# Depthwise convolution begun one stage earlier, with five small moves in the order of the chains

## The chip, the cores and the metric

The kernel runs on one core of a Trainium2 chip. The metric is the time of one execution on the device in microseconds, as the median of several runs. The core has TensorE (PE in the profile), VectorE (DVE), ScalarE (ACT), GpSimd (POOL) and the queue engine SyncE (SP); GpSimd and SyncE do almost nothing here but issue DMA transfers. Each engine works through its own queue in order and waits on semaphores that the others raise.

## The reference

Eight images `x` of 384 channels and 32 x 32 positions go through two layers, all in float32. The first is an attention block on the 1024 positions as tokens, the second a convolution block.

```python
# layer 0, xf = x as (B, 1024, 384)
xn  = layernorm(xf, g1, beta1)
q, k, v = heads(einsum('bnc,oc->bno', xn, w_qkv) + b_qkv)      # 8 heads of 48
out = softmax(q @ k.T * 48 ** -0.5) @ v
x1  = einsum('bnc,oc->bno', out, w_proj) + b_proj + xf
h   = gelu(einsum('bnc,oc->bno', layernorm(x1, g2, beta2), w_fc1) + b_fc1)   # 1536 wide
x2  = x1 + einsum('bnh,oh->bno', h, w_fc2) + b_fc2
# layer 1
y   = depthwise_conv_7x7(x2, dw_w) + dw_b
y   = gelu(layernorm(y, ln_w, ln_b) @ w1 + b1)                  # 1536 wide
gx  = sqrt(sum(y ** 2, positions)); nx = gx / (mean(gx, channels) + 1e-6)
y   = grn_gamma * (y * nx) + grn_beta + y
out = x2 + y @ w2 + b2
```

## The kernel before, in words

The 384 channels of an image lie on the partitions as three channel tiles (`ct` 0 to 2) of 128; the 1024 positions are the free axis, cut in halves of 512 columns, since a matmul writes one 512-column bank of the accumulators. The 1536 hidden channels are 12 tiles `m`.

**The order of TensorE's work.** Image `b` goes through `qk` (queries and keys), attention of its first query half, `proj`, attention of the second query half, fc1 on the first half of the positions, `proj` of the second half, the rest of fc1, fc2; then comes w1 of image `b - 1`, v of image `b + 1`, and w2 of image `b - 1`. So while the matmuls of image `b`'s attention run, the depthwise convolution of image `b - 1` is computed beside them, on VectorE and ScalarE. Image 0 has extra work on the weights (`prepare`, `forms`, `folds`), and image 7 an ending of its own.

**Products of thirds.** `qk`, w1 and part of fc1 use a scheme with fewer products: a group is three output tiles by two column halves, made of 15 products instead of 18, with copies on ScalarE and additions on VectorE between them (`tiles_by_thirds`: matmul L456, ScalarE copies L469 and L477, VectorE additions L472 and L475). w1 has four such groups of 512 columns per image (`grn_up`, tiles `h_*`); fc1 has two groups of 256 columns in the first half of images 2 to 6, called fast (`gelu_group`, tiles `fc_*`; the first covers m = 6 to 8, the second 9 to 11). Their right-hand sides are sums of blocks of the normalised input, made on VectorE (`make_thirds`, L430). fc2 and w2 use a similar scheme on larger sums (`by_thirds`: L485, VectorE L1055, L1052).

**fc1 of a fast image.** First group, m = 0 and 1, `proj` of the second query half, then m = 2 to 5, the second group, and the twelve tiles of the second half of the positions (L404, gelu on ScalarE L497). Ahead of the second group lie the second layernorm's steps for the second half of the positions (`layernorm`: VectorE L540 and L543, a matmul with ones L507, VectorE L550, squares on ScalarE L557, VectorE L561 and L564, L507 again, ScalarE L577 and L578, VectorE L581). ScalarE changes its function table (ACT_TABLE_LOAD, L493 or with L497) between L577's logarithm and a gelu. Products of 256 columns leave a 128x256 tile of the accumulators.

**The convolution** of an image is 49 taps for each channel tile. `convolution` puts one tap of one channel tile after another on VectorE (L1205 for the first tap with its bias, L1207 for the others: `acc = window * weight + acc`); the window is a shifted view of the padded image `pad`, which ScalarE fills by copies of x (L965). `help_convolution` gives the last 6, 7 and 7 taps of the three tiles to ScalarE (L1228) and adds them to `acc` by a DMA that GpSimd issues (L1229). `start_conv` starts both after w1's stage; `conv_norm` and `end_soon` start the third layernorm (`ln3_*`, two halves side by side, `abreast`; sums on 64-row strips, L521) on `acc` in fc1's second half, and `before_fc2` lets `make_thirds` follow. `norm_of_next` normalises the next image (`ln1_*`: sums L1918, VectorE L1938, ScalarE L1940, last scaling L1964).

**What sets the order.** Nothing is scheduled at run time: the Python code writes each engine's queue. `Flow` keeps a clock that every matmul advances by its cost (`U = 0.857` for 512 columns). The side work is written as generators (chains) that yield a wait; once the clock has passed a chain's due time, its next step is put into the queues behind what stands there. A `paced` chain counts its waits from its last due time, others from the present; `flow.finish` emits the rest of a chain at once. `hold` makes the convolution pause while the named stages run. So each number that a chain yields is a place in the queues, not a time on the chip:

```python
start_conv(b, 1.65 if b == B - 2 else 1.95, (23, 2.4), (24, 9.0), (25, 20.0), (84, 1.45))
```

This says 2.4 per tap up to the 23rd tap, 9.0 after the 24th, 20.0 after the 25th, 1.45 up to the 84th and 1.95 from there.

**Buffers.** Ring `p` has three tiles of 128 x 1024, used by attention's probabilities (L812), fc2's and w2's `e` tiles and the squares of w1's stage (`waste`); ring `res` has four tiles of 128 x 512. The accumulators are two double banks (`s_tile`) and four single ones in rotation (`o_tile`); the sums L507 and L521, half of L1918's and fc1's matmuls draw from the four.

**Weights** that image 0 prepares are written to device memory (`s_fc`, `s_fc2`, `s_w1`, `s_w2`) and read back by SP's queue (L328); `weights.release()` lets the loads of the finished ones be issued. The same queue moves attention's sums and their inverses (`average`: L764, L768, L771, L773, L790).

Of the kernel before, what the change touches and what calls it, by code (L numbers as in the profile page):

```python
# [46 lines left out]
F32 = mybir.dt.float32  # L47
# [18 lines left out]
NC = HT // CM  # L66
U = 0.857
HELPED = 6, 7, 7
SCALE = HD ** -0.5
EPS0, EPS1, GRN_EPS = 1e-5, 1e-6, 1e-6  # L70
SUM_LOW, SUM_HIGH = 1e-25, 1e25
# [104 lines left out]
def block_kernel(  # L176
# [42 lines left out]
    def half(h):  # L219
        return slice(h * NH, (h + 1) * NH)  # L220
# [305 lines left out]
    def layernorm(src, dst, h, eps, g, name, switch, spare=None, spaced=False, slow=1.0, fold=None, wait=3.4, gentle=False, late=0, lag=0, fold_squares=True):  # L526

        cols = h if isinstance(h, slice) else half(h)
        if isinstance(h, slice):
            h = h.start
        width = cols.stop - cols.start
        if spare:
            a, *squares = (t[:, :width] for t in spare())
            rstd = a
        else:
            a = one.tile([P, NH], F32, tag="ln_a", name=f"{name}_a{h}")[:, :width]
        nc.vector.tensor_tensor(a, src[:, 0, cols], src[:, 1, cols], ALU.add)  # L540
        if gentle:
            yield 1.2
        nc.vector.tensor_tensor(a, a, src[:, 2, cols], ALU.add)  # L543
        yield 2.6 * slow
        totals = yield from token_sums(a, f"{name}_sum{h}", fold, wait)
        yield 0.8
        for ct in range(CT):
            for total, part in totals:
                to, of = dst[:, ct, cols][:, part], src[:, ct, cols][:, part]
                nc.vector.scalar_tensor_tensor(to, total, -1.0 / C, of, ALU.mult, ALU.add)  # L550
            if gentle:
                yield 1.2
        yield 0.8 * slow + lag
        if not spare:
            squares = [three.tile([P, NH], F32, tag="ln_sq", name=f"{name}_sq{h}_{ct}")[:, :width] for ct in range(CT)]
        for ct in range(CT):
            nc.scalar.activation(squares[ct], dst[:, ct, cols], AF.Square)  # L557
            if spaced:
                yield 1.7
        yield 0.8 if spaced else 1.8 * slow  # L560
        nc.vector.tensor_tensor(squares[0], squares[0], squares[1], ALU.add)  # L561
        if gentle:
            yield 1.2
        nc.vector.tensor_tensor(squares[0], squares[0], squares[2], ALU.add)  # L564
        yield 1.8 * slow
        if not fold_squares:
            fold = None
            yield wait
        totals = yield from token_sums(squares[0], f"{name}_var{h}", fold, wait)
        yield 0.8  # L570

        if not spare:
            rstd = one.tile([P, NH], F32, tag="ln_rstd", name=f"{name}_rstd{h}")[:, :width]
        if switch:
            ln_table()
        for var, part in totals:
            nc.scalar.activation(rstd[:, part], var, AF.Ln, bias=eps, scale=1.0 / C)  # L577
        nc.scalar.activation(rstd, rstd, AF.Exp, scale=-0.5)  # L578
        yield (2.6 if switch else 1.2) * slow + late
        for ct in range(CT):  # L580
            nc.vector.scalar_tensor_tensor(dst[:, ct, cols], dst[:, ct, cols], col(g, ct), rstd, ALU.mult, ALU.mult)  # L581
            if gentle and ct < CT - 1:
                yield 1.2
# [338 lines left out]
                    nc.sync.dma_start(out=other, in_=own)  # L922
                proj("x", xt, qt * P // NH)

    def gelu_half(hid, m, h, xn, weights, wname, name, bank=o_tile):
        w = weights.at(wname, m // CM)[:, m % CM * CT : (m % CM + 1) * CT, :]
        ps = linear_half(lambda k: w[:, k, :], lambda k: xn[:, k, :], CT, h, f"{name}_{h}_{m}", bank)
        other_table(hid[:, m, half(h)], ps, AF.Gelu, bias=bfc1[:, m : m + 1])

    def gelu_group(hid, g, b, weights):  # L930

        tiles = {}

# [11 lines left out]
        def behind(n):  # L945
            if n == 14:
                gelu(2)

        c = {f"c{r + 1}{n + 1}": hid[:, 6 + 3 * g + r, quarter(n)] for r in range(CT) for n in range(2)}
        for _ in tiles_by_thirds(weights, f"fc1t_{b}", g, thirds["fc1"], c, bank, behind, U / 2):  # L950
# [27 lines left out]
    def mlp(b, xt, xn, weights, tag, ln, rest, before_fc2=None, behind_ln=None):  # L978
# [9 lines left out]
        for m in range(HT // 2 if fast else HT):  # L988
            if fast and m == 0:
                hold.append("group")  # L990
                gelu_group(hid, 0, b, weights)
                hold.clear()
            gelu_half(hid, m, 0, xn, weights, wa, f"fc1_{b}")
            if m == (1 if fast else 3) and rest:
                rest()
                slow = 0.8 if fast else 1.2 if b == 1 else 1.0
# [2 lines left out]
                ln = flow.spawn(layernorm(xt, xn, 1, eps0, "g2", f"ln2_{b}", True, slow=slow))  # L999
                behind_ln(ln)  # L1000
        if fast:
            gelu_group(hid, 1, b, weights)
            hold.clear()
        flow.finish(ln)
        for m in range(HT):
# [172 lines left out]
        rows, cols = inside(dy, dx, y0, y1)  # L1178
        return 120 + (rows.stop - rows.start) * (cols.stop - cols.start)

    def convolution(acc, us, first=(), y0=0, y1=H, ready=tuple(range(CT)), taken=None, helped=(0,) * CT):

        done = [0] * CT
        ct, n = None, 0
        taps = [KS * KS - k for k in helped]

# [2 lines left out]
        while any(d < k for d, k in zip(done, taps)):  # L1191
            left = [c for c in ready if done[c] < taps[c] and not (taken and taken.get(c, 0) > flow.now)]
            if not left or hold:
                yield 0.5
                continue
            ct = min([c for c in left if c != ct] or left, key=lambda c: done[c])
            i = done[ct]
            share = shares[i]
            dy, dx = divmod(TAPS[i], KS)
            rows, cols = inside(dy, dx, y0, y1)  # L1200
            window = inner(ct)[:, rows.start + dy - PAD : rows.stop + dy - PAD, cols.start + dx - PAD : cols.stop + dx - PAD]
            dst = image(acc[:, ct, :])[:, rows, cols]
            tap = col("dww", ct * KS * KS + TAPS[i])
# [4 lines left out]
            done[ct] += 1  # L1208
            n += 1
            yield share * next((early for m, early in first if n <= m), us)  # L1210

    def help_convolution(acc, us, taken):

# [18 lines left out]
        yield 8.0  # L1232
        taken.clear()

    def grn_up(b, weights, tag):

# [1 line left out]
        y = one.tile([P, HT * N], F32, tag="big", name=f"y_{b}").rearrange("p (m n) -> p m n", m=HT)  # L1240
        gx = small.tile([P, HT], F32, tag="gx", name=f"gx_{b}")
        waste = three.tile([P, N], F32, tag="p", name=f"h_{b}_squares")

        def gelu(g, r):
            m = g + 4 * (r - 1)
# [333 lines left out]
    def prepare(weights, aside):  # L1579
# [117 lines left out]
        if aside:  # L1697
            yield from shift_through_w1()
            return
        yield from forms("fc2", wfc2, s_fc2)  # L1700
        weights.release()
        yield from shift_through_w2()
        yield from forms("w2", w2, s_w2)

# [86 lines left out]
    def main():  # L1791
# [46 lines left out]
        state = {"help": None, "xn": xn, "conv": None, "acc": None, "norm1": None, "norm3": None}  # L1838
        kept = {}

        def start_conv(b, us, *first):
            acc = state["acc"] = one.tile([P, CT, N], F32, tag="acc", name=f"acc_{b}")
            taken = {}
            state["conv"] = flow.spawn(convolution(acc, us, first, taken=taken, helped=HELPED), paced=True)
            state["help"] = flow.spawn(help_convolution(acc, 2.5, taken), paced=True)

        def conv_norm(b, ln):
# [40 lines left out]

        def end_soon(b):
            end_convolution(b)  # L1890
            yield 18.0 if b > 1 else 22.0

        def norm_of_next(b, us):

# [66 lines left out]
            for h, a, _ in pairs:  # L1961
                for ct in range(CT):
                    part = xn[:, ct, half(h)]
                    nc.vector.scalar_tensor_tensor(part, part, col("g1", ct), a, ALU.mult, ALU.mult)  # L1964
                    yield 1.2

        def before_fc2(b):

# [35 lines left out]
        for b in range(B):  # L2004
# [31 lines left out]
            flow.finish(state["norm3"])  # L2036
            if b < B - 1:
                flow.finish(state["w1"])
                y, gx = grn_up(b - 1, weights, b - 1)
                start_conv(b, 1.65 if b == B - 2 else 1.95, (23, 2.4), (24, 9.0), (25, 20.0), (84, 1.45))  # L2040
                scale = flow.spawn(grn_scale(b - 1, gx, weights, b - 1, y))
                next_values(b + 1)
                flow.finish(scale)
# [176 lines left out]
```

## Time and profile before

| | |
|---|---|
| median of 3 runs | 3253.69 us (3248.43, 3254.41, 3253.69) |
| profiled execution, own time | 3252.55 us |
| its span | 3250.7 us |
| TensorE's granted clock | 0.999 |
| busy share of the span: PE, PEld, DVE, ACT, POOL | 99%, 43%, 78%, 52%, 16% |
| w1's stage, images 1 to 6 (h_n's first matmul to v's first) | 51.88, 53.70, 53.70, 53.70, 53.70, 53.70 us |
| fc1, fast image: first group, second group | 7.00 us, 7.94 us |

PE is TensorE's matmuls, PEld its weight loads, which lie beside the matmuls. A 512-column matmul appears as two records 0.43 us apart, a 256-column one as two 0.22 us apart. The timeline's columns are start, duration, engine, line, operation, out <- in with shapes, the number of instructions, and in brackets the idle time of the engine just before and what ended it. Matmuls are pipelined, so idle time between two records understates what a wait costs; measured from start to start it is some tenths more.

### The profile page before, as it was taken

How to read it: one execution, taken by the hardware profiler on the slowest of the kernel's cores; microseconds unless marked ns; L12 is line 12 of the kernel's file. 1: busy time of each engine (PE TensorE's matmuls, PEld its weight loads, DVE VectorE, ACT ScalarE, POOL GpSimd, SP SyncE). 2: the span in 40 equal slices, each digit the busy share in tenths (PEclk: the TensorE clock that was granted, in tenths of full speed). 3: DMA queues.
4: the chain of work that ended last, by engine and by line, in shares of the span. 5: the costliest groups of instructions: out<-in, count | busy, mean ns of one | idle time of the engine just before them, and what ended most of it. 6: DMA issues, size and time to landing. Idle time of an engine off the chain costs nothing.

```text
span 3250.7 us, 39427 instructions
## 1 busy us (share of the span) xinstructions
PE 3206.4 (99%) x14204; PEld 1402.9 (43%) x14204; DVE 2535.1 (78%) x3578; ACT 1684.0 (52%) x2389; POOL 506.5 (16%) x607
## 2 busy tenths in 40 slices
PE   9999999999999999999999999999999999999999
PEld 5344444443444434444344443444335443344454
DVE  4548888788877888778877788787987778879964
ACT  3542763447644475454753637637375374742543
POOL 2102311112120121201212012120121201200000
PEclk9999999999999999999999999999999999999999
DMA  6535832657445564546636375363843638433244
GB/s 209 176 108 180 171 75 55 157 116 170 91 87 139 134 146 91 107 126 161 130 72 133 106 186 104 76 136 102 196 98 73 136 104 203 74 77 83 66 115 114
DMA packets 208741, 396.77 MB, mean 122 GB/s; under 512 B 42912, under 2 KB 49440, under 8 KB 208160
## 3 DMA queue, kind: packets, MB, share of 16 engines
q0 software_dynamic: 81984, 167.02, 27.0%
q1 hardware_dynamic: 126272, 226.49, 23.4%
q8 instruction: 114, 1.87, 0.2%
q10 hardware_dynamic: 288, 0.71, 0.1%
q14 instruction: 83, 0.68, 0.1%
HBM read 212.98 MB, written 40.11 MB: 78 GB/s over the span
## 4 chain that ended last, share of the span: by engine, by line
PE 75%; DVE 8%; DMA 6%; issue 6%; ACT 3%; POOL 1%; SPq 0%; DVEq 0%; POOLq 0%; ACTq 0%
PE fc L404 13%; PE o L823 11%; PE s L803 11%; PE fc_p L485 7%; PE o_p L485 6%; PE v L723 3%; DMA acc<-tap 3%; PE h_n L456 3%; PE proj L745 3%; PE h_z L456 3%; PE h_x L456 2%; PE o L1315 2%; PE h L391 2%; PE h_last L1364 2%; DVE acc L1207 1%
## 5 line engine op out<-in xcount | busy, mean ns | idle before, releaser
L1207 DVE SCALAR_TENSOR_TENSOR acc<-pad,vec,acc 128x930 f32<-128x930 f32 (+8 forms) x868 | 967.3, 1154 | 5.4 <-DMA acc<-tap 3.2
L812 ACT ACTIVATE p<-s 128x1024 f32<-128x1024 f32 x512 | 523.4, 1024 | 253.1 <-PE s L803 245.5
L803 PE MATMUL s<-qk 48*64 48x512 f32 x4096 | 544.2, 590 | 11.5 <-ACT qk L647 8.6
L823 PE MATMUL o<-p,v 64*64 64x512 f32 x4096 | 541.0, 588 | 0.0
L404 PE MATMUL fc<-xn,fc 128*128 128x512 f32 x972 | 426.0, 593 | 0.0
L1229 POOL DMA_DIRECT2D acc<-tap x280 | 241.2, 878 | 1174.4 <-DVE gscale L1393 426.4
L485 PE MATMUL o_p<-y,w 128*128 128x512 f32 x664 | 289.0, 592 | 0.0
L803 PEld LDWEIGHTS s<-qk 48*64 48x64 f32 x4096 | 163.2, 132 | 288.7 <-issue 206.2
L823 PEld LDWEIGHTS o<-p,v 64*64 64x64 f32 x4096 | 168.4, 132 | 271.9 <-issue 257.1
L404 PEld LDWEIGHTS fc<-xn,fc 128*128 128x128 f32 x972 | 183.7, 190 | 227.7 <-issue 223.4
L485 PE MATMUL fc_p<-qk,fc 128*128 128x512 f32 x520 | 228.9, 595 | 0.5 <-DVE qk L1055 0.4
L1228 ACT ACTIVATE tap<-pad,vec 128x512 f32<-128x512 f32 x280 | 206.4, 738 | 28.7 <-DMA acc<-tap 28.6
L485 PEld LDWEIGHTS o_p<-y,w 128*128 128x128 f32 x664 | 125.6, 190 | 157.7 <-issue 144.0
L1207 DVE SCALAR_TENSOR_TENSOR acc_last<-pad,vec,acc_last 128x377 f32<-128x377 f32 (+24 forms) x288 | 177.2, 690 | 0.6
L485 PEld LDWEIGHTS fc_p<-qk,fc 128*128 128x128 f32 x520 | 97.1, 190 | 128.0 <-issue 114.3
L497 ACT ACTIVATE qk<-fc,bfc_f 128x512 f32<-128x512 f32 x90 | 61.8, 686 | 154.4 <-PE fc L404 154.2
L965 ACT COPY pad<-x 128x512 f32<-128x512 f32 x42 | 26.2, 634 | 207.4 <-DVE x L1055 207.4
L745 PE MATMUL proj<-attn,wproj_sb 128*128 128x512 f32 x288 | 129.0, 602 | 3.7 <-DVE attn L790 3.1
L497 ACT ACTIVATE hid<-fc,bfc_f 128x512 f32<-128x512 f32 x72 | 49.3, 686 | 159.2 <-PE fc L404 159.1
L723 PE MATMUL v<-wv_sb,xn 128*128 128x384 f32 x384 | 126.8, 487 | 0.0
L764 DVE TENSOR_TENSOR attn<-o,attn 128x512 f32<-128x512 f32 x64 | 44.1, 689 | 99.8 <-ACT attn L762 98.7
L472 DVE TENSOR_TENSOR y<-h_n,y 128x512 f32<-128x512 f32 x72 | 49.8, 691 | 62.9 <-PE h_n L456 60.5
(442 smaller groups left out, 4568.5 us busy)
## 6 DMA issues: line engine op xcount, KB each, us to landing
acc<-tap POOLq DMA_DIRECT2D x280, 256.0 KB, 3.7
fc<-s_fc SPq DMA_DIRECT2D x91, 256.0 KB, 2.9
w<-s_w SPq DMA_DIRECT2D x91, 256.0 KB, 2.6
w<-s_w SPq DMA_DIRECT2D x72, 320.0 KB, 2.9
fc<-in_wfc SPq DMA_DIRECT2D x54, 384.0 KB, 4.3
y<-y POOLq DMA_DIRECT2D x38, 512.0 KB, 6.6
qk<-qk POOLq DMA_DIRECT2D x30, 512.0 KB, 7.5
qk<-s_qk SPq DMA_DIRECT2D x42, 320.0 KB, 4.9
```

Of the source, the lines that this page charges most:

```text
L404: nc.tensor.matmul(out=ps, lhsT=lhsT(k), rhs=rhs(k)[:, half(h)], start=(k == 0), stop=(k == nk - 1))
L456: nc.tensor.matmul(out=at, lhsT=weights.at(wname, g, slot // 5)[:, slot % 5, :], rhs=rhs[n], start=first, stop=True, skip_group_check=not ...
L485: nc.tensor.matmul(out=bank, lhsT=lhsT, rhs=rhs, start=k == 0, stop=k == len(pairs) - 1)
L497: nc.scalar.activation(dst, src, function, **kw)
L723: nc.tensor.matmul(out=ps[:, :C], lhsT=xn[:, k, t * P : (t + 1) * P], rhs=wv_sb[:, k, :], start=(k == 0), stop=(k == CT - 1),)
L745: nc.tensor.matmul(out=ps, lhsT=wproj_sb[:, m, ct * P : (ct + 1) * P], rhs=attn[:, m, :], start=(m == 0), stop=(m == CT - 1),)
L803: nc.tensor.matmul(out=s[64 * i : 64 * i + 64, j, :], lhsT=kT[64 * j : 64 * j + HD, m, k0 : k0 + 64], rhs=qT[64 * j : 64 * j + HD, m, half ...
L812: nc.scalar.activation(p, s, AF.Exp)
L823: nc.tensor.matmul(out=outs[i][64 * j : 64 * j + 64, :], lhsT=v[keys, t, at : at + 64], rhs=p[keys, j, :], start=(t == 0), stop=(t == KT - 1),
L1207: nc.vector.scalar_tensor_tensor(dst, window, tap, dst, ALU.mult, ALU.add)
L1228: nc.scalar.mul(t.rearrange("p (h w) -> p h w", w=W), window, tap)
L1229: nc.gpsimd.dma_start(out=acc[:, ct, half(h)], in_=t, accum_op=ALU.add)
```

## The change

1. `begin_convolution` is new. In w1's stage of images 1 to 6 it computes the first five taps (`BEGUN`) of channel tiles 1 and 2 into two tiles of ring `p`, ten VectorE instructions spaced 4.6 apart. `convolution` then starts these two channel tiles with their sixth tap, which reads the held tile and writes `acc`, and goes on from there. `start_conv`'s pauses and cadence change with it.
2. `end_soon` waits 11.0 instead of 18.0 before the third layernorm begins, for images after the first.
3. In fast images the gelu of tile m = 5 of fc1's first half is issued behind the second group's first gelu instead of ahead of the group (`waiting`).
4. In fast images `layernorm`'s pause before its sum is 2.6 instead of 2.08 (`max(slow, 1.0)`).
5. The last scaling of `norm_of_next` (L1964) is spread at 2.4 instead of 1.2.
6. In image 0 `weights.release()` for fc2's prepared weights comes 14.0 later, and the chain that called it goes on without waiting.

```diff
--- before.py
+++ after.py
@@ -66,6 +66,7 @@
 NC = HT // CM
 U = 0.857
 HELPED = 6, 7, 7
+BEGUN = 5
 SCALE = HD ** -0.5
 EPS0, EPS1, GRN_EPS = 1e-5, 1e-6, 1e-6
 SUM_LOW, SUM_HIGH = 1e-25, 1e25
@@ -541,7 +542,7 @@
         if gentle:
             yield 1.2
         nc.vector.tensor_tensor(a, a, src[:, 2, cols], ALU.add)
-        yield 2.6 * slow
+        yield 2.6 * max(slow, 1.0)
         totals = yield from token_sums(a, f"{name}_sum{h}", fold, wait)
         yield 0.8
         for ct in range(CT):
@@ -922,12 +923,18 @@
                     nc.sync.dma_start(out=other, in_=own)
                 proj("x", xt, qt * P // NH)
 
-    def gelu_half(hid, m, h, xn, weights, wname, name, bank=o_tile):
+    def gelu_half(hid, m, h, xn, weights, wname, name, bank=o_tile, later=False):
         w = weights.at(wname, m // CM)[:, m % CM * CT : (m % CM + 1) * CT, :]
         ps = linear_half(lambda k: w[:, k, :], lambda k: xn[:, k, :], CT, h, f"{name}_{h}_{m}", bank)
-        other_table(hid[:, m, half(h)], ps, AF.Gelu, bias=bfc1[:, m : m + 1])
-
-    def gelu_group(hid, g, b, weights):
+
+        def gelu():
+            other_table(hid[:, m, half(h)], ps, AF.Gelu, bias=bfc1[:, m : m + 1])
+
+        if later:
+            return gelu
+        gelu()
+
+    def gelu_group(hid, g, b, weights, waiting=None):
 
         tiles = {}
 
@@ -945,6 +952,8 @@
         def behind(n):
             if n == 14:
                 gelu(2)
+                if waiting:
+                    waiting()
 
         c = {f"c{r + 1}{n + 1}": hid[:, 6 + 3 * g + r, quarter(n)] for r in range(CT) for n in range(2)}
         for _ in tiles_by_thirds(weights, f"fc1t_{b}", g, thirds["fc1"], c, bank, behind, U / 2):
@@ -990,7 +999,7 @@
                 hold.append("group")
                 gelu_group(hid, 0, b, weights)
                 hold.clear()
-            gelu_half(hid, m, 0, xn, weights, wa, f"fc1_{b}")
+            waiting = gelu_half(hid, m, 0, xn, weights, wa, f"fc1_{b}", later=fast and m == HT // 2 - 1)
             if m == (1 if fast else 3) and rest:
                 rest()
                 slow = 0.8 if fast else 1.2 if b == 1 else 1.0
@@ -999,7 +1008,7 @@
                 ln = flow.spawn(layernorm(xt, xn, 1, eps0, "g2", f"ln2_{b}", True, slow=slow))
                 behind_ln(ln)
         if fast:
-            gelu_group(hid, 1, b, weights)
+            gelu_group(hid, 1, b, weights, waiting)
             hold.clear()
         flow.finish(ln)
         for m in range(HT):
@@ -1178,11 +1187,12 @@
         rows, cols = inside(dy, dx, y0, y1)
         return 120 + (rows.stop - rows.start) * (cols.stop - cols.start)
 
-    def convolution(acc, us, first=(), y0=0, y1=H, ready=tuple(range(CT)), taken=None, helped=(0,) * CT):
-
-
-
-        done = [0] * CT
+    def convolution(acc, us, first=(), y0=0, y1=H, ready=tuple(range(CT)), taken=None, helped=(0,) * CT, begun={}):
+
+
+
+        done = [begun[c][1] if c in begun else 0 for c in range(CT)]
+        held = {c: t for c, (t, _) in begun.items()}
         ct, n = None, 0
         taps = [KS * KS - k for k in helped]
 
@@ -1194,10 +1204,18 @@
                 yield 0.5
                 continue
             ct = min([c for c in left if c != ct] or left, key=lambda c: done[c])
+            ct = min(held, default=ct)
             i = done[ct]
             share = shares[i]
             dy, dx = divmod(TAPS[i], KS)
             rows, cols = inside(dy, dx, y0, y1)
+            if ct in held:
+                own, window = image(held.pop(ct)), pad[:, ct, dy : dy + H, dx : dx + W]
+                nc.vector.scalar_tensor_tensor(image(acc[:, ct, :]), window, col("dww", ct * KS * KS + TAPS[i]), own, ALU.mult, ALU.add)
+                done[ct] += 1
+                n += 1
+                yield 1.4
+                continue
             window = inner(ct)[:, rows.start + dy - PAD : rows.stop + dy - PAD, cols.start + dx - PAD : cols.stop + dx - PAD]
             dst = image(acc[:, ct, :])[:, rows, cols]
             tap = col("dww", ct * KS * KS + TAPS[i])
@@ -1208,6 +1226,20 @@
             done[ct] += 1
             n += 1
             yield share * next((early for m, early in first if n <= m), us)
+
+    def begin_convolution(tiles, many, us):
+
+        for i in range(many):
+            dy, dx = divmod(TAPS[i], KS)
+            rows, cols = inside(dy, dx, 0, H)
+            for ct, t in tiles.items():
+                window = inner(ct)[:, rows.start + dy - PAD : rows.stop + dy - PAD, cols.start + dx - PAD : cols.stop + dx - PAD]
+                dst, tap = image(t)[:, rows, cols], col("dww", ct * KS * KS + TAPS[i])
+                if i == 0:
+                    nc.vector.tensor_scalar(dst, window, tap, col("dwb", ct), ALU.mult, ALU.add)
+                else:
+                    nc.vector.scalar_tensor_tensor(dst, window, tap, dst, ALU.mult, ALU.add)
+                yield us
 
     def help_convolution(acc, us, taken):
 
@@ -1232,7 +1264,7 @@
         yield 8.0
         taken.clear()
 
-    def grn_up(b, weights, tag):
+    def grn_up(b, weights, tag, begin=None):
 
 
 
@@ -1240,6 +1272,8 @@
         y = one.tile([P, HT * N], F32, tag="big", name=f"y_{b}").rearrange("p (m n) -> p m n", m=HT)
         gx = small.tile([P, HT], F32, tag="gx", name=f"gx_{b}")
         waste = three.tile([P, N], F32, tag="p", name=f"h_{b}_squares")
+        if begin:
+            begin()
 
         def gelu(g, r):
             m = g + 4 * (r - 1)
@@ -1697,8 +1731,12 @@
         if aside:
             yield from shift_through_w1()
             return
+        def release():
+            yield 14.0
+            weights.release()
+
         yield from forms("fc2", wfc2, s_fc2)
-        weights.release()
+        flow.spawn(release())
         yield from shift_through_w2()
         yield from forms("w2", w2, s_w2)
 
@@ -1838,10 +1876,15 @@
         state = {"help": None, "xn": xn, "conv": None, "acc": None, "norm1": None, "norm3": None}
         kept = {}
 
+        def begin_conv(b):
+            tiles = {ct: three.tile([P, N], F32, tag="p", name=f"begun_{b}_{ct}") for ct in (1, 2)}
+            state["begun"] = {ct: (t, BEGUN) for ct, t in tiles.items()}
+            state["begin"] = flow.spawn(after(None, begin_convolution(tiles, BEGUN, 4.6), 1.0), paced=True)
+
         def start_conv(b, us, *first):
             acc = state["acc"] = one.tile([P, CT, N], F32, tag="acc", name=f"acc_{b}")
             taken = {}
-            state["conv"] = flow.spawn(convolution(acc, us, first, taken=taken, helped=HELPED), paced=True)
+            state["conv"] = flow.spawn(convolution(acc, us, first, taken=taken, helped=HELPED, begun=state.pop("begun", {})), paced=True)
             state["help"] = flow.spawn(help_convolution(acc, 2.5, taken), paced=True)
 
         def conv_norm(b, ln):
@@ -1888,7 +1931,7 @@
 
         def end_soon(b):
             end_convolution(b)
-            yield 18.0 if b > 1 else 22.0
+            yield 11.0 if b > 1 else 22.0
 
         def norm_of_next(b, us):
 
@@ -1962,7 +2005,7 @@
                 for ct in range(CT):
                     part = xn[:, ct, half(h)]
                     nc.vector.scalar_tensor_tensor(part, part, col("g1", ct), a, ALU.mult, ALU.mult)
-                    yield 1.2
+                    yield 2.4
 
         def before_fc2(b):
 
@@ -2036,8 +2079,9 @@
             flow.finish(state["norm3"])
             if b < B - 1:
                 flow.finish(state["w1"])
-                y, gx = grn_up(b - 1, weights, b - 1)
-                start_conv(b, 1.65 if b == B - 2 else 1.95, (23, 2.4), (24, 9.0), (25, 20.0), (84, 1.45))
+                y, gx = grn_up(b - 1, weights, b - 1, lambda: begin_conv(b))
+                flow.finish(state["begin"])
+                start_conv(b, 1.65 if b == B - 2 else 1.85, (23, 2.4), (24, 9.0), (25, 26.0), (72, 1.5))
                 scale = flow.spawn(grn_scale(b - 1, gx, weights, b - 1, y))
                 next_values(b + 1)
                 flow.finish(scale)
```

## The prediction

> **What bounds the kernel now.** I read the page's first two parts, then the table of waits on TensorE, then the timeline of the stages that this table names, then the instruction orders of the two kernels.
>
> ```profile
> span 3250.7 us, 39427 instructions
> ...
> PE 3206.4 (99%) x14204; PEld 1402.9 (43%) x14204; DVE 2535.1 (78%) x3578; ACT 1684.0 (52%) x2389; POOL 506.5 (16%) x607
> ```
>
> TensorE is the bound in every stage, and about 44 us of its span are idle. The change removes no matmul, so it can win only idle time, and the most it can lose is what it puts in front of a matmul. The table of waits (engine, line, what it waited for: us in all, times, longest) splits the idle time:
>
> ```profile
> PE h_n L456 <- ACT y L477: 8.8, 5, 1.8
> PE s L803 <- ACT qk L647: 8.6, 7, 2.1
> PE fc_n L456 <- ACT qk L477: 4.9, 5, 1.0
> PE ln_sum L507 <- DVE ln_a L543: 3.3, 5, 0.9
> PE proj L745 <- DVE attn L790: 3.1, 1, 3.1
> ```
>
> "Five times" is images 2 to 6. Three rows are the change's targets: h_n (start of w1's stage), fc_n (fc1's second group), ln_sum (second layernorm's sum). VectorE at 78% is the other engine to watch: it carries the moved taps.
>
> **A. ln2's sum, one matmul later.** For images 2 to 6 slow is 0.8, so the pause after L543 goes from 2.08 to 2.6 planner units, and the sum is put one matmul (0.86 us: two records 0.43 apart) later. From one matmul's start to the next it now loses 0.91, 1.10, 0.76, 0.77 and 0.54 us; up to 0.86 of each goes, 3.8 in all. **-3.8.**
>
> **B. The deferred gelu.** Image 3's second group, before, first ScalarE and then VectorE:
>
> ```profile
> 1309.49 1.28 ACT L497 ACT_TABLE_LOAD   x1
> 1310.79 0.69 ACT L497 ACTIVATE qk<-fc,bfc_f 128x512 f32<-128x512 f32 x1
> 1311.37 0.36 ACT L477 COPY qk<-fc_n 128x256 f32<-128x256 f32 x1
> 1311.62 0.39 ACT L477 COPY qk<-fc_k 128x256 f32<-128x256 f32 x1
> ```
>
> ```profile
> 1309.51 2.08 DVE L581 SCALAR_TENSOR_TENSOR xn<-xn,vec,ln_rstd 128x512 f32<-128x512 f32 x3 [5.05 <-ACT ln_rstd L578]
> 1312.04 0.42 DVE L472 TENSOR_TENSOR qk<-fc_x,qk 128x256 f32<-128x256 f32 x1 [0.46 <-ACT qk L477]
> ```
>
> The group's first copy stands behind a table load and the gelu of tile 5; TensorE loses 1.14 us per image there by starts (the group takes 7.94 us, the first group 7.00). With the gelu moved behind the second group's gelus the copies can run at once: 1.28 + 0.69 us leave their way, and the five small copies and L469 that it is moved past lose nothing. Taken alone this is -5.7 over five images. But A moves the variance too, and in the changed order ln2's three L581 no longer stand ahead of the group's adds: they stand between the first L472 and the second. Counting from the group's first matmul: x is done at 1.45, its copies at 1.44, first L472 at 1.49; L581 at 1.82, 2.48 and 3.14 (0.66 apart); second L472 from 3.80 to 4.22, and the seventh product, which reads it, is wanted at 2.59. That is a stall of 1.66 instead of 1.14. Bounds: -5.7 if VectorE gets the L581s out of the way, +2.6 by this count; I take **+2.6**, because the order is written out. [...]
>
> **C. Third layernorm sooner.** end_soon starts it 11 planner units after the convolution's end, not 18. Fast images now make the thirds (L430) at fc2's end, between its adds, and VectorE comes late to w1's stage, whose first copies stand behind four pad copies. Before, image 3:
>
> ```profile
> 1404.04 0.68 DVE L1055 TENSOR_TENSOR fc_spare<-fc_n,fc_spare 128x512 f32<-128x512 f32 x1
> ...
> 1406.02 1.88 DVE L1055 TENSOR_TENSOR x<-fc_p,x 128x512 f32<-128x512 f32 x3
> ```
>
> ```profile
> 1406.74 1.83 ACT L965 COPY pad<-x 128x512 f32<-128x512 f32 x3 [0.63 <-DVE x L1055]
> 1408.47 0.57 ACT L477 COPY y<-h_n 128x512 f32<-128x512 f32 x1
> ```
>
> ```profile
> 1409.10 1.12 PE L456 MATMUL h_n<-attn,w 128*128 128x512 f32 x2 [1.77 <-ACT y L477]
> ```
>
> TensorE loses 1.93 us by starts; the stage is 53.70 us long, and image 1's, where nothing is late, 51.88. In the changed order all L430 stand before the eighteenth product of fc2. Then the last x adds end 1.4 us after the stage starts, the last pad copies run 0.9 to 2.2, the h_n copy 2.1 to 2.7, against 2.57 wanted: 0.1 is left. 5 x 1.8: **-9.0** (bounds -9.6 and 0).
>
> **D. Ten taps inside w1's stage (images 1 to 6).** Two tensor_scalar and eight scalar_tensor_tensor per image stand among the group adds; as many leave the starts of the next stages (in the order five fewer L1207 stand in qk's stage and five fewer in fc1's tail; none is added, since the sixth tap's merge is a tap too). VectorE was busy 35.5 us of this stage's 53.7; ten taps add 2 x 0.8 + 8 x 1.09, 10.3 us, so it holds them. What counts is where each stands. The adds (0.69 us) follow products 0.86 apart, and most are not needed at once; a tap costs only when it is directly ahead of an add whose bank or sum is the next product's. Laying the order out with the rows' durations I find one such place, the 21st product, for 0.12 us: 6 x 0.12, **+0.7**. No trace of before has a tap there. The upper bound takes each tap directly ahead of an urgent add: it costs its 1.09 less one product's 0.86, 0.23, ten of them 2.3 per image, 14 in all. A gain has no reason: no product is waiting for less. The two tiles take ring-p buffers that fc2's fc2_e tiles held, last read by the 36th of fc2's 68 matmuls, so that no tap waits for its buffer.
>
> **E. A new wait in fc1's second half.** With C, ln3's sums (L521) come in after tile 9's first matmul and ln1's sums (L1918) directly behind them; before, ln1's came first and ln3's after tile 11:
>
> ```profile
> 944.02 0.71 PE L1918 MATMUL ln_sum<-ln,ones 32*128 32x256 f32 x8
> 944.66 7.13 PE L404 MATMUL fc<-xn,fc 128*128 128x512 f32 x16
> 951.73 0.65 PE L521 MATMUL ln_sum<-ln_a,ones 64*64 64x512 f32 x2
> ```
>
> ```profile
> 952.85 3.68 DVE L550 SCALAR_TENSOR_TENSOR acc<-ln_sum,acc 128x512 f32<-128x512 f32 x6 [3.59 <-PE ln_sum L521]
> ```
>
> The ring of four banks gives ln1's last sum the bank of ln3's first, which three L550 must have read. From ln3's first matmul: L550 starts at 1.12, its third ends at 1.12 + 2 x 0.60 + 0.68, about 3.0. ln1's last sum is wanted at 1.01 + 0.48, 1.5. A stall of 1.55 per image, and fc1's tiles 9 to 11 are queued behind it; the next bank, freed by the sixth L550 at 4.8, is wanted at 4.9. 5 x 1.55: **+7.8** (bounds +10 with that second bank late, 0 if the L550s are read off sooner). [...]
>
> **F. The rest.** Small stalls in fc2 (0.2 four times, 0.54 once) and at the start of qk (0.18 five times, VectorE behind taps that now stand elsewhere): **-1.9**, at worst 0. The 8.6 us at qk's end are ScalarE copies behind the helper's taps, whose order stays: 0, give or take 3. s_fc2's loads moved 14 units later clear SP's queue for image 0's transfers; the one proj wait (3.1) follows from the head m = 1, whose back move was issued behind VectorE's sums_singly, not behind these loads: 0 (-3.1 to +1). ln1's last scaling is spread over 14 us instead of 7 and is still done some 20 us before v reads it: 0.
>
> **Sum.** -3.8 + 2.6 - 9.0 + 0.7 + 7.8 - 1.9 = -3.6 us. The profiled run's own time is 3252.55 (span 3250.7 and 1.85 around it), 1.1 below the median 3253.69; it becomes 3249.0, and on the median's scale 3250.1. I say 3250.
>
> **Rivals.** First, the two new waits do not bite (L581 finished before the second L472 is due, L550s quicker): the sum loses 2.6 + 5.7 and 7.8 and is about -20, time 3234; with only E gone, -11, 3242. For it: each has only some 1.6 us to make up. Against: both follow from order in queues, not from durations. Second, slower: the taps in w1's stage come in front of urgent adds, D's upper price 14 instead of 0.7, sum about +10, 3263; it decides the sign once a stage loses over 0.7 us, three taps. For it: no row shows such a mixture, and many of w1's adds feed the next add. Against: VectorE idles a third of that stage. Third, the change does not do what it says: the first begun tap, which waits for pad copies, stands ahead of the first h_x add, so VectorE is still late, and h_n's 1.9 stays: sum +5.4, 3259.
>
> **How the numbers follow.** This kernel can be told from no change at about 0.2%, 6.5 us: below 3247.2 is faster, above 3260.2 slower. The forecast has 0.40, the first rival 0.27, the second 0.20, the third 0.13. Of the forecast's 0.40, 0.05 falls below 3247.2 (the qk-end stall of F shorter) and 0.02 above 3260.2; of the first rival's 0.27, 0.01 stays within; of the second's 0.20, 0.03, since part of its price is enough for no change; of the third's 0.13, 0.08. Faster 0.05 + 0.26 = 0.31; slower 0.02 + 0.17 + 0.05 = 0.24; same 0.45. The range from 3236 to 3264 leaves out the first rival's far half and what lies beyond the second's price. The forecast's own range is 3244 to 3257.
>
> **What would show it.** Right: ln_sum L507 gone from the waits; fc_n waiting for VectorE's L472 in the second group at 1.5 to 1.9; ln_sum L1918 waiting for L550 at 1.3 to 1.8, five times; w1's stages of images 2 to 6 near 52.0 us. Wrong: w1's stages still 53 or more, with TensorE waiting for L472 or L475 behind taps (second or third rival), or no wait at L1918 and fc_n (first).

## The result, and the profile after

Over 12 runs of each the changed kernel takes 3244.16 us (median; 3238.9 to 3248.88) and the kernel before 3252.36 (3244.06 to 3254.46): ratio 0.9978, 95% interval 0.9969 to 0.9987, or 7 us less (4 to 10). The forecast was 3250, 3.6 us less, in a range from 3236 to 3264; the sign and the range hold, the measured gain is about twice the forecast, and at 0.22% it lies just beyond the 0.2% that the forecast called no change.

Line numbers from here on are those of the changed file: before's L404, L456, L472, L477, L507, L521, L550, L581, L647, L745, L790 and L803 are one higher, L1207 is L1225 and L1918 is L1961. The page's first part of the kernel after:

```profile
span 3243.9 us, 39415 instructions
...
PE 3213.5 (99%) x14204; PEld 1402.6 (43%) x14204; DVE 2540.3 (78%) x3578; ACT 1683.6 (52%) x2389; POOL 506.5 (16%) x607
```

The span is 6.8 us shorter, yet TensorE is busy 7.1 us longer for the same 14204 matmuls. Some of them ran slower, which the table of waits cannot show: the mean granted clock is 0.997 of full speed against 0.999 before, which over 3244 us is some 6 us. That table, after (engine, line, what it waited for: us in all, times, longest):

```profile
PE s L804 <- ACT qk L648: 8.6, 7, 2.4
PE fc_n L457 <- DVE qk L473: 8.0, 5, 1.6
PE ln_sum L1961 <- PE ln_sum L1961: 1.7, 5, 0.4
...
PE proj L746 <- DVE attn L791: 0.5, 1, 0.5
PE ln_sum L508 <- DVE ln_a L544: 0.3, 1, 0.3
```

h_n's wait is gone and ln_sum L508's nearly; fc_n's has grown and changed its releaser from ScalarE to VectorE's L473; a small new one stands at ln1's sums, which the profile puts down to the sum ahead of it and not to a VectorE instruction.

The surest reading is a ledger: the time from a stage's first matmul to the next stage's, kernel against kernel. (The stage and group times ahead of the prediction run to the end of the last matmul and are 0.16 us longer: 53.70 there is 53.53 here, 51.88 is 51.72, 7.94 is 7.78. The forecasts of the experiments use that measure in places.) Summed over the images:

| stretch | forecast | one profile against the other |
|---|---|---|
| A: tiles 2 to 5 with ln2's sum | -3.8 | -4.0 |
| B: second group (7.78 to 8.45) | +2.6 | +3.4 |
| C: w1's start, images 2 to 6 | -9.0 | -9.0 |
| D: taps in w1's stage, 6 x 0.45 | +0.7 | +2.7 |
| E: fc1's tail (32.85 to 36.45, 36.50, 34.81, 34.83, 36.45) | +7.8 | +14.8 |
| F: fc2 | -1.0 | -5.6 |
| F: qk and attention | -0.9 | -3.9 |
| release: image 0's proj | 0 | -4.3 |
| start and end of the kernel | 0 | -0.8 |
| sum | -3.6 | -6.8 |

C and D share w1's stage (53.53 to 52.17 in images 2 to 6). Image 1's stage, which had no late start, went from 51.72 to 52.17, and that is D. The qk and attention row contains a loss too: in image 7's qk the granted clock was 0.50 from 2736.65 to 2743.48, which by an estimate from these two figures is 3.4 us; before has nothing of the kind there. The release row is one pair of profiles, and the experiments show how little one pair says of it.

**B** in image 3, VectorE and then TensorE:

```profile
1305.54 0.42 DVE L473 TENSOR_TENSOR qk<-fc_x,qk 128x256 f32<-128x256 f32 x1 [5.61 <-PE fc_x L457]
1305.88 2.06 DVE L582 SCALAR_TENSOR_TENSOR xn<-xn,vec,ln_rstd 128x512 f32<-128x512 f32 x3
1307.86 0.41 DVE L473 TENSOR_TENSOR qk<-fc_n,qk 128x256 f32<-128x256 f32 x1
```

```profile
1308.33 0.70 PE L457 MATMUL fc_n<-xn,fc1t 128*128 128x256 f32 x2 [1.61 <-DVE qk L473]
```

The three L582 stand between the first and the second add, and the seventh product waits for the second, 1.61 us of idle time or 1.77 by starts (the forecast's measure): the forecast said 1.66. The group grew by 0.67 per image, where the forecast had 0.52.

**E** in image 3, TensorE and VectorE:

```profile
1336.54 1.08 PE L522 MATMUL ln_sum<-ln_a,ones 64*64 64x512 f32 x4
1337.60 1.08 PE L522 MATMUL ln_sum<-attn,ones 64*64 64x512 f32 x4
1338.61 0.71 PE L1961 MATMUL ln_sum<-ln,ones 32*128 32x256 f32 x6
1339.65 0.67 PE L1961 MATMUL ln_sum<-ln,ones 32*128 32x256 f32 x2 [0.34 <-PE ln_sum L1961]
1340.25 8.83 PE L405 MATMUL fc<-xn,fc 128*128 128x512 f32 x16
```

```profile
1337.67 3.68 DVE L551 SCALAR_TENSOR_TENSOR acc<-ln_sum,acc 128x512 f32<-128x512 f32 x6 [7.74 <-PE ln_sum L522]
```

Three things stand in these lines. The last pair of ln1's sums starts at 1339.65, 3.11 us after ln3's first matmul and 0.1 after the third L551 is through: the predicted bank wait. The second pair of ln3's sums (attn) runs after the first instead of beside it: in before all eight records started in two bursts 0.48 apart. Its fold, a DMA that GpSimd issues at 1331.28 behind two others, lands at 1337.47 in the trace, 0.1 us before the pair starts. This lateness costs nothing of its own, because it passes while the bank is still held: in the six kernels with this order of sums the second pair comes 0.95 to 1.15 us late, and the last pair starts 3.10 or 3.11 us after ln3's first matmul in all 30 tails. And the 16 records of fc1 behind the sums take 8.83 us, where before's L404 row after ln1's sums has 7.13. The view by windows shows why (each sum stretch and the 4 us behind it, image 3 and image 4):

```profile
core 0: us, PE busy (x) PEld busy (x) DVE busy (x) ACT busy (x) POOL busy (x), PEclk, DMA share, GB/s
1336.50:1340.20 3.70, 3.36 (x17) 1.02 (x16) 2.53 (x5) 0.00 (x0) 0.00 (x0) 1.00 0.19 63
1340.20:1344.20 4.00, 4.00 (x7) 1.65 (x7) 4.00 (x9) 1.70 (x3) 0.00 (x0) 0.57 0.00 0
1734.60:1738.30 3.70, 3.35 (x17) 1.02 (x16) 2.56 (x5) 0.00 (x0) 0.00 (x0) 1.00 0.18 60
1738.30:1742.30 4.00, 4.00 (x11) 1.82 (x11) 4.00 (x9) 2.23 (x4) 0.00 (x0) 1.00 0.23 58
```

Behind the same 3.7 us of sums the granted clock fell to 0.57 over 4 us in image 3 (4.0 x 0.43 = 1.7 us lost) and not in image 4. Images 2, 3 and 6 have such a stretch: 3 x 1.65 of E's 14.8 us.

**F** in fc2: before, ln1's variance sums waited in a bank for ScalarE's L577; the first fence is before, the second after.

```profile
1367.52 1.54 PE L1918 MATMUL ln_var<-ln,ones 32*128 32x256 f32 x8
```

```profile
1367.39 0.71 PE L1961 MATMUL ln_var<-ln,ones 32*128 32x256 f32 x8
```

In before the last pair of these starts at 1368.36, when ScalarE's first L577 (1367.62, 0.69 us long) is through. With ln3's variance now ahead by several products the wait of 0.8 us is gone, 5 times, and some 0.2 of small stalls at fc2's adds with it.

### The profile page after: what moved, and what is told of

The parts are those of the page before. It is cut to its first block, busy times and chain, and to the rows that moved or that the text cites. A ratio compares the mean times of both kernels' runs of the same rounds, so it can differ in the third digit from the quotient of the medians.

```text
span 3243.9 us, 39415 instructions
## 1 busy us (share of the span) xinstructions
PE 3213.5 (99%) x14204; PEld 1402.6 (43%) x14204; DVE 2540.3 (78%) x3578; ACT 1683.6 (52%) x2389; POOL 506.5 (16%) x607
## 4 chain that ended last, share of the span: by engine, by line
PE 86%; issue 5%; DMA 4%; DVE 3%; ACT 1%; POOL 1%; SPq 0%; POOLq 0%; DVEq 0%; ACTq 0%
PE fc L405 15%; PE s L804 13%; PE o L824 12%; PE fc_p L486 11%; PE o_p L486 6%; PE v L724 4%; PE proj L746 4%; PE h_n L457 3%; DMA acc<-tap 3%; PE h_z L457 3%; PE h_x L457 3%; PE h_last L1398 2%; PE o L1349 2%; PE h L392 2%; PE h_k L457 1%
## 5 line engine op out<-in xcount | busy, mean ns | idle before, releaser
L1225 DVE SCALAR_TENSOR_TENSOR acc<-pad,vec,acc 128x930 f32<-128x930 f32 (+8 forms) x808 | 905.5, 1157 | 5.7 <-DMA acc<-tap 2.5
L1225 DVE SCALAR_TENSOR_TENSOR acc_last<-pad,vec,acc_last 128x377 f32<-128x377 f32 (+24 forms) x288 | 177.2, 688 | 0.6
L486 PEld LDWEIGHTS fc_p<-qk,fc 128*128 128x128 f32 x520 | 98.4, 190 | 123.6 <-issue 119.1
L724 PEld LDWEIGHTS v<-wv_sb,xn 128*128 128x128 f32 x384 | 72.5, 190 | 50.1 <-issue 3.3
```

Source lines behind the costliest of these rows:

```text
L486: nc.tensor.matmul(out=bank, lhsT=lhsT, rhs=rhs, start=k == 0, stop=k == len(pairs) - 1)
L724: nc.tensor.matmul(out=ps[:, :C], lhsT=xn[:, k, t * P : (t + 1) * P], rhs=wv_sb[:, k, :], start=(k == 0), stop=(k == CT - 1),)
L1225: nc.vector.scalar_tensor_tensor(dst, window, tap, dst, ALU.mult, ALU.add)
```

## The experiments

Each starts from the changed kernel unless it says otherwise. The first seven have one profiled execution each and are read by stage, where w1's stage and the second group repeat to some 0.01 us from image to image; the kernel with both edits and the last two were timed 6, 11 and 6 times. The first theory was that of the prediction: each stretch has its own cause, and they add. The rivals stand in the expectations.

**The release undone.**

```diff
-        flow.spawn(release())
+        weights.release()
```

> The changed kernel with its sixth part undone: s_fc2's loads are released at once again. Theory: image 0's second-half wait at proj (before 3.1 us, after 0.5) hangs on these loads. SP has them in its queue ahead of the move of head group m = 3's sums, and the idle time is followed by a stretch at half clock (0.58 over 4 us in before, 1.7 us lost). Then from proj's start to fc1 in image 0 the time goes back from 53.1 to 57.4 us (plus 4.3), the rest of the ledger stays, span near 3248. Rival, the prediction's own term: the wait comes from head group m = 1 behind VectorE's sums and does not hang on the loads; the stretch stays near 53 us (within 0.5) and the span near 3244.

Measured: image 0's stretch from proj to fc1 57.18 us (53.11 in the changed kernel), as the theory said; but the span was 3240.6, not 3248, mainly because no half-clock stretch fell into fc1's tails in this run (34.80 in all five images). And three other kernels with the same image 0 and the later release have 55.06, 58.41 and 52.65 in their profiles. One profile does not settle this term; the last two runs take it up.

**ln2's sum at its old place.**

```diff
-        yield 2.6 * max(slow, 1.0)
+        yield 2.6 * slow
```

> The changed kernel with its fourth part undone: ln2's pause before its sum is 2.08 again in images 2 to 6. Theory: in the second group it is VectorE's three L581, queued behind the first L472, that hold TensorE; with the sum one matmul earlier the L581 stand ahead of the group, and the group takes about 7.4 us instead of 8.61 (stall 0.4 instead of 1.6), while the wait at the sum itself comes back (0.5 to 1.1 per image, 4.0 in all). Net for images 2 to 6: about minus 2. Rival: the group's stall is still ScalarE's copies; the group stays at 8.6 and the change is plus 4.

Measured: second group 7.23 instead of 8.45 us in all five images; tiles 2 to 5 longer by 0.73, 0.97, 0.99, 0.52 and 0.45. Net 3.7 - 6.1 = -2.4. So in the second group it was VectorE's order, and A's gain of some 4 was paid for with 6. Without A the deferred gelu brings the group from before's 7.78 to 7.23, 2.7 us in all and not the 5.7 that the prediction gave it when taken alone: the L581, now ahead of the group's adds, still delay its sixth product by 0.46 us by starts.

**The gelu ahead of the group.**

```diff
-            waiting = gelu_half(..., later=fast and m == HT // 2 - 1)
+            waiting = gelu_half(..., later=False)
```

> The changed kernel with its third part undone: the gelu of tile 5 stands ahead of the second group again. Theory: ScalarE's first copy waits again for table load and gelu (1.1 to 1.2 us) and VectorE's L581 come on top of that, since they stand behind the L472 that waits for this copy: the second group goes from 8.61 to about 9.8 us, plus 1.2 in each of five images, plus 6 in all. Rival: the two waits overlap (both measured from the group's start), the group stays at about 8.6 and the deferral brought nothing.

Measured: 9.57 us in all five images, 1.12 more each. The waits of this kernel show that the two stalls add:

```profile
PE fc_n L457 <- DVE qk L473: 7.4, 5, 1.5
PE fc_n L457 <- ACT qk L478: 4.9, 5, 1.0
```

The deferral does its work in the changed kernel; the layernorm's new place hid it.

**No taps in w1's stage** (`begin_conv` not called, `start_conv` with the numbers of before).

```diff
-                y, gx = grn_up(b - 1, weights, b - 1, lambda: begin_conv(b))
-                flow.finish(state["begin"])
-                start_conv(b, ... 1.85, (23, 2.4), (24, 9.0), (25, 26.0), (72, 1.5))
+                y, gx = grn_up(b - 1, weights, b - 1)
+                start_conv(b, ... 1.95, (23, 2.4), (24, 9.0), (25, 20.0), (84, 1.45))
```

> The changed kernel with its first part undone: no taps in w1's stage, the convolution's cadence and pauses as before. Theory: w1's stage falls by the 0.45 us that image 1's stage gained, to 51.9, in images 1 to 6 (minus 2.7 in all); the ten taps go back to the starts of qk and fc1's tail, qk's stages lose about 0.5 us each again. Rival: without the ten taps moved out, the convolution is later at its end, the third layernorm starts later, and w1's first stall (1.9) returns in images 2 to 6: stage 53.7, plus 7.

Measured: w1's stage 51.71 in all six images, so the taps cost the 0.45 and the rival falls. The stretch from qk to proj has a mean of 98.4 us over images 2 to 7, against 97.7 in the changed kernel. It varies from image to image, so I pool: three kernels without the begun taps (before, this one, the release alone) have means 98.2, 98.4 and 98.7; the nine with them 96.7 to 97.9, mean 97.4. Half-clock stretches make part of the scatter. With half their length taken off, an estimate from the traces' granted clock, the three have 98.2, 97.8 and 97.5, the nine 96.7 to 97.5, mean 97.1. So some 0.8 us per image is gained in the next qk. fc1's tail is longer without the taps as well: 35.10 to 35.17 in its three images at full clock, against 34.80. Against this stand 0.45 per image spent in w1's stage. The begun taps are worth some 3 us by this estimate, which rests on pooled single profiles.

**The third layernorm late again.**

```diff
-            yield 11.0 if b > 1 else 22.0
+            yield 18.0 if b > 1 else 22.0
```

> The changed kernel with its second part undone: the third layernorm begins 18 planner units after the convolution's end again. Theory: the early third layernorm pays at w1's start and costs in fc1's tail. w1's stage goes from 52.17 to about 53.9 us in images 2 to 6 (plus 1.8 each, plus 9), fc1's tail to fc2's start from 34.8 to 32.9 with no half-clock stretch behind it, fc2 from 53.56 to 54.6: per image plus 0.9, and minus 1.65 wherever the profile of the changed kernel had a half-clock stretch. Rival: w1's stage keeps its 52.2 because the ten begun taps, not the layernorm, relieved VectorE there.

Measured: w1's stage 54.46 in images 2 to 6 (expected 53.9), fc1's tail 32.85 in all, fc2 54.61. The wait is back where it was:

```profile
PE h_n L457 <- ACT y L478: 8.9, 5, 1.8
PE fc_n L457 <- DVE qk L473: 8.1, 5, 1.6
```

So the earlier layernorm, not the taps, relieved w1's start, and E is its price: per image -2.3 in w1 and -1.05 in fc2, +1.95 in the tail, and 1.65 more where the clock falls. With the late layernorm and the taps the stage is 0.93 longer than before's (54.46 against 53.53), twice the 0.45 that the taps cost with the early one: C and D do not simply add.

**L581 ahead of the second group's adds** (L582 in this file).

```diff
-                ln = flow.spawn(layernorm(xt, xn, 1, eps0, "g2", f"ln2_{b}", True, slow=slow))
+                ln = flow.spawn(layernorm(xt, xn, 1, eps0, "g2", f"ln2_{b}", True, slow=slow, late=-1.3 if fast else 0))
```

> The changed kernel with one edit: ln2's last pause in images 2 to 6 is 0.8 planner units instead of 2.08, so that the three L581 stand ahead of the second group's adds, while the sum stays one matmul late and the gelu deferred. Theory: both waits are gone at once; the second group takes about 7.3 us (stall 0.3 instead of 1.6) and the stretch of tiles 2 to 5 stays at 12.0: minus 1.2 in each of five images, minus 6 in all. Rival: the L581 then delay the group's first L472 by as much as they delayed the second, and the group stays near 8.5.

Measured: 7.24 us in all five images, tiles 2 to 5 at 12.0 to 12.6. VectorE and TensorE in image 3:

```profile
1304.84 2.08 DVE L582 SCALAR_TENSOR_TENSOR xn<-xn,vec,ln_rstd 128x512 f32<-128x512 f32 x3 [4.20 <-ACT ln_rstd L579]
1306.83 0.42 DVE L473 TENSOR_TENSOR qk<-fc_x,qk 128x256 f32<-128x256 f32 x1
```

```profile
1307.30 0.70 PE L457 MATMUL fc_x<-qk,fc1t 128*128 128x256 f32 x2 [0.30 <-DVE qk L473]
```

The same three instructions, one place earlier in VectorE's queue, use time in which it was idle; TensorE waits 0.30 instead of 1.61.

**ln1's sums ahead of ln3's.**

```diff
-            yield 11.0 if b > 1 else 22.0
+            yield 12.0 if b > 1 else 22.0
-                    state["norm1"] = ... norm_of_next(b, 22.0 if b > 1 else 28.0)
+                    state["norm1"] = ... norm_of_next(b, 17.0 if b > 1 else 28.0)
```

> The changed kernel with two numbers altered: ln1's sums come 5 planner units sooner (17 instead of 22), the third layernorm one unit later (12 instead of 11), so that ln1's sums stand some six matmuls ahead of ln3's. Theory: ln1's last sum no longer waits for the L550s to read a bank that ln3's sum holds, and ln3's second pair no longer waits for its fold's landing; fc1's tail goes from 34.8 (36.5 with half clock) to about 32.9 us, fc2 stays at 53.6, w1's stage at 52.2 to 52.4, and no half-clock stretch follows in any of five images: minus 10 against a profile with none, minus 15 against the changed kernel's. Rival: the wait only moves to ln3's sums, whose banks ln1's L1938 then hold, and the tail stays near 34.8.

Measured: fc1's tail 32.96 in all five images, no half-clock stretch in any, fc2 53.56; w1's stage 52.85, 0.68 more than the changed kernel's (the forecast allowed 0.2). The rival falls. The part of the theory on the fold is not tested here, since both waits go at once; the constant 3.11 above speaks against it. The gain over the changed kernel's tails is 3.5, 3.5, 1.9, 1.9 and 3.5, less 3.4 in w1: 11 us. The one execution has a span of only 3239.0, because image 0's stretch was 59.07 in it and half-clock stretches fell into three qk stages.

**Both edits.**

> The changed kernel with both edits: L581 ahead of the second group, and ln1's sums ahead of ln3's. Theory: the two gains add, minus 6 and minus 10 to 15, since they lie in different stages; w1's stage may give back some tenths (its adds move against the taps). Time near 3228 where the changed kernel has 3244, ratio to before near 0.9930. Rival: what TensorE no longer waits for in fc1 it waits for in fc2, w1 or the next qk, where VectorE is late; ratio 0.9970 or more.

Measured: 3227.71 us (3223.76 to 3231.5, 6 runs), ratio to before 0.9928, interval 0.9914 to 0.9943. This beats both kernels, before by 23 us and the changed one (0.9978, interval 0.9969 to 0.9987, from an earlier session) by 16. So the rival, that the waits only move, does not hold. Its waits:

```profile
PE s L804 <- ACT qk L648: 6.3, 7, 1.3
PE fc_x L457 <- DVE qk L473: 1.5, 5, 0.3
PE s L804 <- ACT p L813: 1.1, 3, 0.5
```

and ln3's sums, run four abreast again, with fc1 at full speed behind them:

```profile
1330.77 0.65 PE L522 MATMUL ln_sum<-ln_a,ones 64*64 64x512 f32 x2
1330.79 0.65 PE L522 MATMUL ln_sum<-attn,ones 64*64 64x512 f32 x2
...
1331.79 6.28 PE L405 MATMUL fc<-xn,fc 128*128 128x512 f32 x14
```

**The release by itself**, first on the kernel before, then taken out of the kernel with both edits (the diff of the first experiment, forwards and backwards).

> The kernel before with the sixth part of the change alone: s_fc2's loads released 14 units later in image 0. In eight profiles with the later release the stretch from image 0's proj to fc1 took 52.7 to 59.1 us (mean 55.2), in two with the release at once 57.2 and 57.4. Theory: the later release is worth about 2 us on average and cannot be read from one profile; ratio to before 0.9994, between 0.9985 and 1.0. Rival: it is worth the 4.3 us of the first comparison; ratio 0.9987 or less.

> The kernel with both edits, but with s_fc2's loads released at once. Where nothing else waits long any more, image 0's stretch is most of the scatter. Theory: about 2 us slower than the kernel with both edits, ratio to before near 0.9934. Rival: 4 us or more, ratio 0.9941 or more; or no difference, 0.9928.

Measured: ratio to before 0.9990, interval 0.9981 to 0.9999, for the release alone (3 us less); 0.9941, interval 0.9924 to 0.9958, without it in the kernel with both edits, against 0.9928 with it (4 us, but the intervals overlap). Image 0's stretch over all profiles: with the later release nine values from 52.7 to 59.1, mean 55.0; with the release at once 57.2, 57.4 and 60.3. The runs point to a gain of 3 us give or take 3; that the later release is worth nothing is excluded only narrowly.

## Why the prediction was right, and where it was not

**Right by its own steps.** A was -4.0 where -3.8 was forecast. B's surprise, that a fix on ScalarE would turn into a wait for VectorE because A pushes the three L581 behind the first add, came as worked out (1.66 forecast, 1.77 measured by starts). One experiment that moves only the L581 removes it, and another that moves the whole chain with the sum does so too. A is right as a sum only: by image it gained 1.0, 1.2, 0.3, 0.8 and 0.6. C came to the tenth (-9.0); with the taps in place it is worth 2.3 per image, as the late layernorm showed. E's new bank wait came in all five images, though the sign that was named for it, a wait for L550 of 1.3 to 1.8 in the table, did not: the table has 0.3 to 0.4, put down to the sum ahead, and only the starts show the rest. The two "new waits do not bite" cases of the first rival are refuted, and so is the third rival: w1's start no longer waits. The second rival put 14 us on the taps; they cost 2.7 in w1's stage.

**Mis-sized: E.** At full clock the tail grew by 1.95 per image, not 1.55. The end of the wait was right: the third L551 ends 3.0 us after ln3's first matmul, as worked out. Its beginning was not. The step counted ln1's last sum as wanted 0.48 us behind ln1's first, but in before all of ln1's sums run beside each other (eight records in 0.71 us), so the last is wanted at the same time as the first, and the wait is longer by that 0.48; the tail shows 0.4 of it. The half-clock stretches, 5 us in this profile, were not in the sum at all, though before's own profile has one: behind the 3.07 us wait at proj the 14 records took 7.97 us, in the changed kernel, after 0.48, 6.28. The prediction counted that wait and not what followed it.

**Mis-sized: D.** 0.12 per stage was forecast, 0.45 measured, inside the bounds. Image 1, VectorE and then TensorE:

```profile
623.54 1.08 DVE L1241 SCALAR_TENSOR_TENSOR begun<-pad,vec,begun 128x841 f32<-128x841 f32 x1
624.55 0.68 DVE L473 TENSOR_TENSOR y<-h_n,y 128x512 f32<-128x512 f32 x1
```

```profile
624.28 1.02 PE L457 MATMUL h_x<-thirds,w 128*128 128x512 f32 x2
625.28 1.12 PE L457 MATMUL h_n<-acc,w 128*128 128x512 f32 x2
```

The matmul starts 1.00 after the one before it instead of 0.86, and takes 0.10 longer itself: here a wait of 0.14 costs 0.24. The same happens once more, behind the 38th product, where the tap at 637.42 costs 0.10 and then another 0.10. These two places make the 0.45; the prediction found the first, counted half of it, and not the second.

**Mis-sized: F.** fc2's -5.6 against -1.0: the table of waits does not list the wait of ln1's variance, and I did not cost ScalarE's hold on its bank, which the same move of ln3 undoes. (The small stalls that F lists add up to 2.2, where its sum has 1.9.) qk's gain of about 1 us per image against 0.15: I priced only VectorE's direct stalls at qk's start. Which wait the rest of this gain comes from was not traced.

**Wrong: the release.** Taken at 0 with a bound of -3.1; the pair of profiles gave -4.3 and the timed runs -3. The step that failed is the one that traced proj's wait to head group m = 1 alone and did not follow SP. In before, VectorE has the sums of m = 3 ready at 99.02, and SP issues their move only at 103.97, behind the loads; in the changed kernel the two times are 98.03 and 98.06, and every later move of the heads is queued behind this one. That is not the whole cause. In the nine kernels with the later release SP issues this move between 97.0 and 98.2, yet the wait at proj is below 0.9 us in five of them and 2.4 to 3.8 in four (2.9, 3.1 and 4.7 with the release at once). What else sets it stays open.

That the total came near is partly luck, because the misses have both signs: D and E cost 9 us more than forecast, F and the release brought 12 more.

## What to carry to other kernels

A fix moves the next instruction in some queue: work out which one is next before counting the gain, and check what stands ahead of it on the engine that releases it; here a later sum gained some 4 us and pushed three VectorE instructions into the worst place, which cost 6, and one number cured it. When a matmul that ran beside others has to wait for a bank, count its wait from the time at which the others start (0.48 us sooner in E). And where several short waits and small matmuls come together, price the clock behind them as well as the waits (here 1.65 to 1.75 us in nine of 30 tails and 3.4 in one).

## What the runs showed of the hardware

The granted clock sometimes falls to half (0.50) behind, or in the last 0.3 us of, a stretch of some 3.7 us in which TensorE is, by the records, busy 3.36 of 3.70 us, but with 64x64 and 32x128 matmuls and one gap of 0.34. In the six kernels that keep the changed kernel's order of sums this happened in 10 of 30 fc1 tails, with a loss of 1.65 to 1.75 us in nine and 3.4 in one; in the six profiles in which the sums stand apart (those of before and of the release alone among them), in none of 30. What decides it in one image and not in the next was not found. In the changed kernel's three tails (images 2, 3 and 6) the granted clock was 0.50 for 3.41 us each time, from 941.24, 1340.60 and 2528.43; the longest idle time of TensorE in the sums there was 0.36, 0.34 and 0.34 us.
